# Query numbers of 16 of 25 edge groups: gathered by GpSimd from DRAM instead of selected on TensorE and VectorE

## The chip, the cores and the metric

The kernel runs on one core of a Trainium2 chip. The metric is the device time of that core in microseconds (us), the median over several runs. Engines are named as the profile does: PE (TensorE), DVE (VectorE), ACT (ScalarE), POOL (GpSimd) and SP (SyncE, which here only issues DMAs and reads registers).

## The reference: what is computed

Two layers of a relational graph attention network run over 3125 nodes of 768 features and 53125 edges (with one loop per node); each edge has one of three types. After them come a residual and a layer norm:

```python
xr = jnp.einsum('nd,rdf->rnf', x, W)        # every node's features by every relation's weights
oi = xr[etype, dst]; oj = xr[etype, src]
qi = oi @ q; kj = oj @ k
alpha = jax.nn.leaky_relu(qi + kj, NEG_SLOPE)
e = jnp.exp(alpha - segment_max(alpha, dst)[dst])
a = e / (segment_sum(e, dst)[dst] + EPS)
out = segment_sum(a * oj, dst) + b          # by head; 4 heads in layer 1, one in layer 2
```

The edges come sorted by their target `dst`. The term `qi` depends on an edge's target and its type alone: for each edge of layer 1 it is 4 numbers (one per head), taken from a table of 3125 nodes x 3 relations x 4 heads. How each edge gets its 4 numbers is what the change is about.

## The kernel before

The edges are cut into 25 groups (NB) of whole target nodes, at most 128 nodes each. A group has 17 slots (SL; 14 in the first, SLF) of 128 edges, one edge per partition. The kernel has three stages. The first stage multiplies x by layer 1's weights. The second gathers the products' rows by edge, weighs and sums them per node, and multiplies by layer 2's weights. The third does the same for layer 2's edges and ends with the norm.

**The products of the first stage.** The products of x and W1 are made 128 nodes at a time, in 6 pieces of up to 398 columns; the last piece carries, beside features, the 12 query numbers (4 heads x 3 relations) of each node. A piece is 18 matmuls (six blocks of features, high and low parts) into one of two PSUM banks. `d_row` (L579) empties the bank: ACT copies it (L581), SP stores it to the table `tab1`. For the last piece DVE also splits the 12 query numbers into three bf16 parts (`split3`, L586), which SP stores to `q1_d` in DRAM.

**The order of the work.** `phase1` (L601) is written as a list of steps: `when(n, f, ...)` puts work at step n, and one piece of the products runs at each step, so a node group has six steps. The order on each engine is exactly the order of these calls; there is no scheduler behind it. At a step the listed work is issued first, then the piece's matmuls, then `d_row` of the piece before. Work that waits on an engine holds up all that stands behind it on that engine.

**Indices.** `a_index`, `a_index2` and `c_next` (L608 to L653) read the edge list of group b at steps 5b+11 and 5b+12, turn it so that each edge sits on its partition, and leave in SBUF the row number for the gathers (`ridx`), the target's place within the group (`dl`) and the type (`rel`).

**Query numbers before.** For each group b, SP loads the targets of all 2176 edges broadcast over 128 partitions (`s_load1`, 544 KB into `sT`) and the group's 128 rows of `q1_d` (`q_load1`). DVE compares `sT` with each partition's node number (`a_q`, L680), which gives one-hot columns in bf16. PE multiplies each slot's one-hot block by the 36 query parts of the nodes (`a_q2`, 17 small matmuls, tile `pq`). DVE makes a one-hot of the type (`a_oh`, L686), multiplies (L708) and sums (L711) into `pall[:, b]`, the 4 numbers of each edge. The second stage's `alpha` (L874) adds them to the key numbers.

**What else hangs on GpSimd in this stage.** 18 blocks of layer 2's weights W2 are prepared on the way. `w_load(i)` at step 12 + 6i issues one or two loads from GpSimd into the single buffer `share[3]` (L745). `w_split(i)` two steps later copies the block's high part on ACT (L752), subtracts on DVE for the low part (L753) and makes two products with q2 and k2 on DVE (L756); the copies are there for blocks 0 to 11 only. Blocks 4 to 11 are stored by a DMA from GpSimd (L759), blocks 0 to 3 by SP. The next load waits until DVE is done with the buffer. After the first stage GpSimd issues all the gathers of table rows (L468), 128 rows of 3,088 bytes per instruction.

The lines that fix where things stand:

```python
k = (q, q, q, q + 3, q + 3, q + 4, q + 5)      # q = max(c + 1, 6 * b + 2), c = 10 + 5 * b
for n, f in zip(k, (s_load1, q_at, q_load1, a_q, a_oh, a_q2, a_q3)):
    when(n, f, b)
...
when(6 * (2 + i), w_load, i)
when(6 * (2 + i) + 2, w_split, i)
```

Of the kernel before, what the change touches and what calls it, by code (L numbers as in the profile page):

```python
# [9 lines left out]
F32 = mybir.dt.float32  # L10
# [3 lines left out]
I32 = mybir.dt.int32  # L14
AF = mybir.ActivationFunctionType
ALU = mybir.AluOpType
# [5 lines left out]
P = 128  # L22
# [4 lines left out]
BIG = float(2**100)  # L27
# [35 lines left out]
def _index(ap):  # L63
    return bass.IndirectOffsetOnAxis(ap=ap, axis=0)
# [3 lines left out]
SL = 17  # L68
# [41 lines left out]
def kernel(  # L110
# [21 lines left out]
    nc = tc.nc  # L132
    N, D = x.shape
    R = layers[0]["W"].shape[0]
    E = src.shape[0]
    NB = (N + P - 1) // P
    NP = NB * P
# [3 lines left out]
    H1 = l1["H"]  # L141
# [5 lines left out]
    HW = RW // 2  # L147
    EARLY = 6
    GB = NB - 4
# [4 lines left out]
    V, S, G, T = nc.vector, nc.scalar, nc.gpsimd, Counted(nc.tensor)  # L154
    OOB = float(1 << 20)

    dram = ctx.enter_context(tc.tile_pool(name="fdram", bufs=1, space=DRAM))
# [6 lines left out]
    tab2 = dram.tile([NP * R, RW], F32, name="ftab2")  # L164
    xb_d = dram.tile([NP + P, D], F32, name="xb_d")
    q1_d = dram.tile([NP + P, H1 * R * 3], BF, name="q1_d")
    w2_d = dram.tile([R * DT * P, 2 * D], F32, name="w2_d")

    ident = keep.tile([P, P], F32, name="fident")
# [26 lines left out]
    pall = keep.tile([P, NB, SL, H1], F32, name="pall")  # L196
# [258 lines left out]
    def slots(b):  # L455
        return SL if b else SLF
# [122 lines left out]
    def d_row(o, q, b, p, po):  # L579

        S.copy(o[:, :HW], po[:, :HW])  # L581
        to = tab1[b * P * R:(b + 1) * P * R, :].rearrange("(p r) f -> p r f", r=R)
        nc.sync.dma_start(to[:, p // 2, p % 2 * HW:(p % 2 + 1) * HW], o[:, :HW])
        if p == len(PIECES1) - 1:
            q1s = q.tile([P, H1 * R, 3], BF, name="q1s", bufs=2)
            split3([q1s[:, :, i] for i in range(3)], po[:, HW:HW + H1 * R], q, [P, H1 * R])  # L586
            nc.sync.dma_start(q1_d[b * P:(b + 1) * P, :], q1s.rearrange("p k s -> p (k s)"))

    def stretches(rows, at_, a, e):

# [10 lines left out]
    def phase1(pre, work, psum, left, due, more):  # L601
        st = a_st
# [13 lines left out]
        def a_index2(b):  # L616
            pT = st[b]["pi"]
            c = SL
            V.tensor_scalar(dl[:, b, :], pT[:, c:2 * c], 1.0 / BIG, n_all[:, b:b + 1], op0=ALU.mult,
                            op1=ALU.subtract)  # L620
            inv = work.tile([P, SL], F32, name="inv", bufs=2)
            V.tensor_scalar(inv, dl[:, b, :], float(P), OOB, op0=ALU.is_ge, op1=ALU.mult)
            V.tensor_add(ridx[:, b, :], pT[:, 0:SL], inv)
            if b in first_rows:
                V.tensor_scalar(rfirst[:, first_rows[b], :], ridx[:, b, :], NP * R - 1, None, op0=ALU.min)
            V.tensor_copy(rel[:, b, :], pT[:, 2 * c:3 * c])

        counts = work.tile([32, 32], F32, name="counts", bufs=1)
        V.memset(counts, 0.0)
# [52 lines left out]

        def a_oh(b):
            s = st[b]
            s["oh"] = work.tile([P, SL, R * 3], F32, name="oh", bufs=2)
            V.tensor_tensor(s["oh"], rel[:, b, :, None].to_broadcast([P, SL, R * 3]),  # L686
                            rel3.rearrange("p r s -> p (r s)")[:, None, :].to_broadcast([P, SL, R * 3]),
                            op=ALU.is_equal)
# [81 lines left out]
        def when(n, f, *a):  # L770
            ev.setdefault(n, []).append((f, a))

        TAIL = 6 * (GB - 1)
        S0 = 10
        when(8, pad_rows)
        for b in range(NB):
            c = S0 + 5 * b
            when(c - 3 if b else S0 - 1, c_load, work, b)
# [4 lines left out]
            q = max(c + 1, 6 * b + 2)  # L783
            if b < GB:
                k = (q, q, q, q + 3, q + 3, q + 4, q + 5)
            else:
                q = max(c + 2, 6 * GB + 4 + 2 * (b - GB))
                e = 6 * NB - 5 + b - GB
                k = (q, 6 * NB - 14 + b - GB, 6 * NB - 5, q + 5, e, e, e)
            for n, f in zip(k, (s_load1, q_at, q_load1, a_q, a_oh, a_q2, a_q3)):  # L790
                when(n, f, b)
            if b > 1:
                t, e = {2: (2, 4), 3: (3, 10), GB: (TAIL - 8, TAIL - 3), GB + 1: (TAIL - 7, TAIL), GB + 2: (TAIL - 6, TAIL - 2), GB + 3: (TAIL - 5, TAIL - 1)}.get(
                    b, (6 * b - 11, 6 * b - 8))
# [1345 lines left out]
```

## Time and profile before

| | |
|---|---|
| time, median of 3 runs | 1773.26 us (1772.15 to 1775.79) |
| the profiled execution | 1773.27 us, span 1771.5 us |
| PE, DVE, ACT, POOL busy | 1649.9, 1122.2, 434.6, 903.6 us |
| mean granted clock of PE | 0.974 |
| from 100 to 400 us: PE, DVE, ACT, POOL busy of 300 us | 300.0, 202.6, 63.6, 15.2 |
| small query products in the first stage (`pq`) | 425 recorded, 177 to 213 ns each by record, pipelined |
| first gather of the second stage begins at | 534.4 us |

The span runs from the first to the last instruction of the profiled execution. A row of the page's second part cuts the span into 40 slices of 44.3 us; the first stage takes the first twelve. A row of a timeline gives start, length, engine, line, operation and tiles, and in brackets how long the engine sat idle before it and what ended that. A row of the groups by line gives the count, then busy time and mean length, then idle time before and what ended it. "SPq" and the like is the engine's instruction queue, where DMAs are issued.

### The profile page before, as it was taken

How to read it: one execution, taken by the hardware profiler on the slowest of the kernel's cores; microseconds unless marked ns; L12 is line 12 of the kernel's file. 1: busy time of each engine (PE TensorE's matmuls, PEld its weight loads, DVE VectorE, ACT ScalarE, POOL GpSimd, SP SyncE). 2: the span in 40 equal slices, each digit the busy share in tenths (PEclk: the TensorE clock that was granted, in tenths of full speed). 3: DMA queues.
4: the chain of work that ended last, by engine and by line, in shares of the span. 5: the costliest groups of instructions: out<-in, count | busy, mean ns of one | idle time of the engine just before them, and what ended most of it. 6: DMA issues, size and time to landing. Idle time of an engine off the chain costs nothing. (4 is left out here: it accounts for less than half of the span.)

```text
span 1771.5 us, 38682 instructions
## 1 busy us (share of the span) xinstructions
PE 1649.9 (93%) x14093; PEld 1272.7 (72%) x14093; DVE 1122.2 (63%) x3912; ACT 434.6 (25%) x803; POOL 903.6 (51%) x907
## 2 busy tenths in 40 slices
PE   8999999999993999999999999938999999999996
PEld 8899999999992788888888888813444444444443
DVE  7566677566425666666677777366666666666662
ACT  6222222111210112221121221102333333333331
POOL 4100000000007777777777776067777777777750
PEclk9999999999996999999999999968999999999998
DMA  7576667556578999999999998478999999999960
GB/s 258 189 242 225 213 219 238 202 169 211 180 260 279 335 347 356 349 351 355 348 341 351 347 347 297 144 259 305 330 338 334 342 336 334 336 337 334 336 224 28
DMA packets 169366, 501.53 MB, mean 283 GB/s; under 512 B 39890, under 2 KB 82489, under 8 KB 169166
## 3 DMA queue, kind: packets, MB, share of 16 engines
q0 software_dynamic: 70832, 343.91, 54.9%
q1 hardware_dynamic: 90104, 144.97, 24.6%
q10 hardware_dynamic: 8230, 10.10, 1.7%
q8 instruction: 112, 1.84, 0.4%
q14 instruction: 88, 0.72, 0.1%
HBM read 414.04 MB, written 89.63 MB: 284 GB/s over the span
## 5 line engine op out<-in xcount | busy, mean ns | idle before, releaser
L468 POOL DMA_INDIRECT extra<-ftab,ridx x296 | 302.7, 1023 | 93.4 <-issue 53.0
L53 PE MATMUL po<-waH,hT 128*128 128x386 f32 (+1 forms) x1200 | 326.4, 347 | 1.4 <-DVE hT L1031 0.7
L53 PE MATMUL po<-waH,xT 128*128 128x386 f32 x1104 | 293.7, 342 | 0.9 <-ACT xT L255 0.4
L468 POOL DMA_INDIRECT share<-ftab,ridx x204 | 207.1, 1015 | 66.9 <-issue 38.9
L53 PEld LDWEIGHTS po<-waH,hT 128*128 128x128 f32 x1200 | 216.7, 189 | 4.8 <-DVE hT L1031 1.1
L53 PE MATMUL D<-extra,AT 128*128 128x512 f32 (+1 forms) x600 | 217.8, 501 | 1.3 <-ACT AT L1400 1.3
L53 PEld LDWEIGHTS po<-waH,xT 128*128 128x128 f32 x1104 | 203.1, 189 | 1.4 <-DVE xT L256 0.7
L53 PE MATMUL po<-waL,hT 128*128 128x386 f32 (+1 forms) x600 | 203.1, 339 | 0.0
L53 PE MATMUL po<-waL,xT 128*128 128x386 f32 x552 | 187.9, 340 | 3.1 <-DVE wbH L416 3.0
L581 ACT COPY share<-po 128x386 f32<-128x386 f32 x150 | 72.2, 481 | 369.5 <-PE po L53 305.0
L53 PEld LDWEIGHTS D<-extra,AT 128*128 128x128 f32 x600 | 107.1, 191 | 73.0 <-issue 65.4
L53 PE MATMUL acc<-waH,marks 128*32 128x386 f32 (+1 forms) x868 | 152.7, 494 | 0.7 <-DVE marks L1320 0.7
L53 PE MATMUL acc<-waL,marks 128*32 128x384 f32 (+1 forms) x848 | 151.7, 498 | 0.0
L53 PE MATMUL po<-wbH,xT 128*128 128x386 f32 (+1 forms) x552 | 147.6, 342 | 0.9 <-DVE g L410 0.9
L53 PE MATMUL acc<-extra,sel 128*32 128x193 f32 x2736 | 124.9, 335 | 2.3 <-DVE sel L940 2.3
L468 POOL DMA_INDIRECT waL<-ftab,ridx x108 | 109.0, 1010 | 32.9 <-issue 27.1
L468 POOL DMA_INDIRECT waH<-ftab,ridx x104 | 105.1, 1010 | 31.7 <-issue 25.3
L53 PE MATMUL acc<-extra,marks 128*32 128x384 f32 (+1 forms) x568 | 116.0, 492 | 0.0
L53 PEld LDWEIGHTS po<-waL,hT 128*128 128x128 f32 x600 | 113.4, 189 | 0.0
L53 PEld LDWEIGHTS acc<-extra,sel 128*32 128x32 f32 x2736 | 87.8, 112 | 31.3 <-issue 5.1
L745 POOL DMA_DIRECT2D share<-in_L_gnn_W_dram x24 | 12.8, 537 | 188.5 <-DVE w2j L756 117.0
L53 PE MATMUL acc<-share,marks 128*32 128x386 f32 (+1 forms) x428 | 108.8, 488 | 0.0
(286 smaller groups left out, 2981.7 us busy)
## 6 DMA issues: line engine op xcount, KB each, us to landing
ftab<-share SPq DMA_DIRECT2D x150, 193.0 KB
ftab<-r SPq DMA_DIRECT2D x50, 386.0 KB
sT<-dr_d SPq DMA_DIRECT2D x23, 544.0 KB
xb_d<-share SPq DMA_DIRECT2D x25, 384.0 KB
ftab<-y SPq DMA_DIRECT2D x100, 96.0 KB
share<-xb_d SPq DMA_DIRECT2D x25, 384.0 KB
share<-in_x_dram SPq DMA_DIRECT2D x24, 384.0 KB
out_dram<-share SPq DMA_DIRECT2D x24, 384.0 KB
```

The source lines that it names most:

```text
L53: return self.add(self.engine.matmul(to, weights, moving, **more), to, moving)
L468: return G.indirect_dma_start(out=to, out_offset=None, in_=tab, in_offset=_index(i[:, j:j + 1]), bounds_check=NP * R - 1, oob_is_err=False)
L581: S.copy(o[:, :HW], po[:, :HW])
L745: G.dma_start(w2[i][p:p + n], l2["W"][r, at:at + n, :])
```

## The change

For groups b below 20 with b % 5 != 4 (16 groups: 0 to 3, 5 to 8, 10 to 13, 15 to 18), the one-hot path is left out: no `s_load1`, `q_at`, `q_load1`, `a_q`, `a_oh`, `a_q2`, `a_q3`. Instead:

- Every node group's 12 query numbers are also copied in float32 with the relation outermost (`q1f`), and stored by SP as 3 rows of 4 numbers per node to a new DRAM table `q1r_d`.
- `a_index2` makes for the 16 groups one more index, target x 3 + type, moved out of range for an edge that is not the group's.
- Per slot one indirect DMA on GpSimd reads 128 rows of 16 bytes from `q1r_d` straight into `pall[:, b, j, :]`. Out-of-range edges are skipped, which is why `pall` is cleared first, at step 8.
- The gathers of a group stand at steps max(6b+9, c+3) to 6 later, two or three to a step. At a step that also has a `w_load` or `w_split`, the gathers stand ahead of it.
- The type's one-hot `oh` has one buffer instead of two.

```diff
+    q1r_d = dram.tile([NP * R, H1], F32, name="q1r_d")
...
+            q1f = q.tile([P, R, H1], F32, name="q1f", bufs=2)
+            V.tensor_copy(q1f, po[:, HW:HW + H1 * R].rearrange("p (h r) -> p r h", h=H1))
+            nc.sync.dma_start(q1r_d[b * P * R:(b + 1) * P * R, :].rearrange("(p r) h -> p r h", r=R), q1f)
...
+            if by_gather(b):
+                d = work.tile([P, SL], F32, name="qd", bufs=2)
+                V.scalar_tensor_tensor(d, pT[:, c:2 * c], R / BIG, pT[:, 2 * c:3 * c], op0=ALU.mult, op1=ALU.add)
+                st[b]["qi"] = work.tile([P, SL], I32, name="qi", bufs=7)
+                V.tensor_add(st[b]["qi"], d, inv)
+
+        def by_gather(b):
+            return b < GB - 1 and b % 5 != 4
+
+        def q_gather(b, j):
+            n = (b + 1) * P * R
+            G.indirect_dma_start(out=pall[:, b, j, :], out_offset=None, in_=q1r_d[:n, :],
+                                 in_offset=_index(st[b]["qi"][:, j:j + 1]), bounds_check=n - 1, oob_is_err=False)
...
-            s["oh"] = work.tile([P, SL, R * 3], F32, name="oh", bufs=2)
+            s["oh"] = work.tile([P, SL, R * 3], F32, name="oh", bufs=1)
...
+        when(8, G.memset, pall, 0.0)
...
-            for n, f in zip(k, (s_load1, q_at, q_load1, a_q, a_oh, a_q2, a_q3)):
-                when(n, f, b)
+            if by_gather(b):
+                for j in range(slots(b)):
+                    when(max(6 * b + 9, c + 3) + j * 7 // SL, q_gather, b, j)
+            else:
+                for n, f in zip(k, (s_load1, q_at, q_load1, a_q, a_oh, a_q2, a_q3)):
+                    when(n, f, b)
```

## The prediction

> **What bounds the kernel now.** I read the page's share lines first, then the windows view cut by stage, and then, inside the first stage, the timelines of PE, ScalarE, VectorE and GpSimd. The chain of waits begins near 1140 us, so it says nothing of the stage that is changed; only two of its rows serve below, for how long a gather takes to land. A measurement of this kernel tells a change from none at about 0.2%, 3.5 us.
>
> ```profile
> span 1771.5 us, 38682 instructions
> PE   8999999999993999999999999938999999999996
> POOL 4100000000007777777777776067777777777750
> 100.00:400.00 300.00, 300.00 (x1932) 297.22 (x1931) 202.58 (x723) 63.62 (x118) 15.19 (x29) 1.00 0.67 217
> 700.00:1140.00 440.00, 436.36 (x5104) 378.35 (x5103) 304.85 (x857) 88.63 (x192) 303.23 (x297) 1.00 0.93 331
> ```
>
> The two last rows give, for a stretch, the busy time of PE, its weight loads, DVE, ACT and POOL, then the granted clock, the DMA share and GB/s. From 100 to 400 us, inside the first stage, PE has no idle time at a clock of 1.00. VectorE is busy 203 of 300 us and GpSimd 15. So what the change takes from VectorE is worth nothing by itself, and what it takes from PE counts in full, as long as nothing new makes PE wait. GpSimd looks free, and that is what has to be tested.
>
> **What PE is spared.** Per gathered group 17 small products go.
>
> ```profile
> 189.92 0.34 PE L53 MATMUL po<-waH,xT 128*128 128x386 f32 x1
> 190.10 0.59 PE L53 MATMUL pq<-q,sT 128*128 128x36 bf16 x17
> 190.54 0.43 PE L53 MATMUL po<-wbH,xT 128*128 128x386 f32 x1
> 220.22 0.48 ACT L581 COPY share<-po 128x386 f32<-128x386 f32 x1 [2.71 <-PE po L53]
> 220.59 0.84 ACT L752 CAST w2hl<-share 128x768 fp32r<-128x768 f32 x1
> 223.38 0.48 ACT L581 COPY share<-po 128x386 f32<-128x386 f32 x1 [1.95 <-issue]
> 227.06 0.48 ACT L581 COPY share<-po 128x386 f32<-128x386 f32 x1 [3.20 <-PE po L53]
> ```
>
> The 17 run from 190.10 to 190.54, 0.44 us. These are rows of the timelines of PE and ScalarE. ScalarE's copies of finished pieces, which follow PE, stand 3.16 us apart in the first pair (220.22 to 223.38) and 3.68 in the next, which holds such a set: 0.5 us. I take 0.49: 16 x 0.49 = 7.9 us, at least 16 x 0.44 = 7.0. If nothing else mattered, the profiled execution's own time, 1773.27 us (1.8 around its span, and the median of the runs but for 0.01), would become 1765.4.
>
> **What VectorE and SP get.**
>
> ```profile
> L680 DVE TENSOR_SCALAR sT<-sT,cols 128x2176 bf16<-128x2176 bf16 x22 | 17.1, 777 | 1.5 <-DMA sT<-dr_d 1.5
> L708 DVE TENSOR_TENSOR tq<-pq,oh 128x324 f32<-128x324 f32 (+1 forms) x42 | 18.0, 469 | 8.1 <-PE pq L53 8.1
> L711 DVE TENSOR_REDUCE pall<-tq 128x68 f32<-128x612 f32 x21 | 16.6, 791 | 0.7
> L686 DVE TENSOR_TENSOR oh<-rel,rel 128x153 f32<-128x153 f32 x21 | 6.6, 314 | 0.0
> 98.23 0.17 DVE L626 COPY rel<-pi 128x17 f32<-128x17 f32 x1
> 98.86 0.18 DVE L207 CAST q1s<-po 128x12 bf16<-128x12 f32 x1 [0.46 <-ACT share L581]
> ```
>
> A gathered group loses 0.78 + 2 x 0.47 + 0.79 + 0.31 = 2.8 us of VectorE. It gains two 17-wide operations like the last but one row (0.2 us each), and every group gains one copy of 12 numbers (0.2 us). All of that lies under PE, as VectorE is a third idle. The new copy reads the product bank after the five steps of the split, so the bank comes free some 0.6 us later; PE wants it one piece, 3.2 us, after the product ended, and this eats slack only (nothing; up to 0.3 us a group, 7 us, where VectorE is late anyway). SP loses 32 loads, and gains 25 stores of about 0.35 us of issue: nothing. The clearing of the gathered numbers (1,700 a partition, on GpSimd) stands ahead of the first weight load; that load is issued at 88.8 us and first read at 101.9, which covers it.
>
> **What GpSimd gets.** 16 groups x 17, less 3 for the short first one: 269 indirect gathers.
>
> ```profile
> 535.79 1.05 POOL L468 DMA_INDIRECT share<-ftab,rfirst  x1 [0.30 <-issue]
> 537.14 1.00 POOL L468 DMA_INDIRECT share<-ftab,rfirst  x1 [0.31 <-issue]
> 538.44 1.00 POOL L468 DMA_INDIRECT share<-ftab,rfirst  x1 [0.30 <-DMA share<-ftab,rfirst]
> L468 POOL DMA_INDIRECT extra<-ftab,ridx x296 | 302.7, 1023 | 93.4 <-issue 53.0
> 36.51 0.53 POOL L288 DMA_DIRECT2D dr_d<-padb  x1
> 185.19 1.05 POOL L745 DMA_DIRECT2D share<-in_L_gnn_W_dram  x2 [1.04 <-DVE w2j L756]
> 202.99 0.57 POOL L759 DMA_DIRECT2D w_d<-w2hl  x1 [16.75 <-DVE w2hl L753]
> ```
>
> The trace has no gather of 16-byte rows. Its gathers of 3,088-byte rows start 1.30 us apart when nothing holds them (537.14 to 538.44): 1.00 of work and a gap of 0.30; over 296 of them work and gap make (302.7 + 93.4) / 296 = 1.34. GpSimd's plain DMAs take about 0.53 us whether they move half a kilobyte (dr_d) or 384 KB (in two halves, L745), so the bytes of a row should not matter, but the instruction. Bounds for one gather: 0.53 (a plain one) and 1.34. I take 1.30, because it is the same instruction with the same 128 indices. 17 x 1.30 = 22.1 us a group.
>
> The next rows are from the groups by line, the timelines and the chain of waits. A group of products takes PE
>
> ```profile
> L752 ACT CAST w2hl<-share x12: 836/837/837, 101.9 to 319.5; 128x768 fp32r<-128x768 f32 x12
> 161.50 0.84 ACT L752 CAST w2hl<-share 128x768 fp32r<-128x768 f32 x1
> 187.71 0.96 DVE L732 TENSOR_TENSOR share<-share 128x768 f32<-128x768 f32 x1 [1.90 <-DMA share<-in_x_dram]
> 183.30 0.35 SPq L728 DMA_DIRECT2D share<-in_x_dram  x1
> 1174.34 4.53 DMA waL<-ftab,rfirst
> 1240.77 6.38 DMA waL<-ftab,ridx
> ```
>
> (319.5 - 101.9) / 11 = 19.8 us, and 19.3 once the small products are gone. So in four groups of five GpSimd needs more time than PE. It can't make it up ahead, for GpSimd's queue also holds the loads of W2's blocks (L745) and, for blocks 4 to 11, the stores of their parts (L759). What queues behind a late load: ScalarE's copy of block i (L752), which stands in ScalarE's order ahead of the copies that empty the product banks, and those hold PE, which has two banks. The copy of 220.59 could start as late as about 225.3 (bank wanted at 226.5, less 0.84 and 0.48, which overlap by 0.1): it may be 4.7 us late before PE stalls. A load of 384 KB takes 4.4 us from issue to use (183.30 to 187.71), and gathers of 395 KB took 4.5 and 6.4; I take 4.8.
>
> Burst one, groups 0 to 3. GpSimd can begin when group 0's index is made, 98.4 plus the two new operations, 98.8. By the steps of the diff 14 + 17 + 17 gathers and the first 8 of group 3, and the loads of blocks 1 and 2, precede the load of block 3: 56 x 1.30 + 2 x 0.53 = 73.9. With 0.5 for the load and 4.8 to land, block 3 is there at 178.0. Its copy stood at 161.5; four sets of small products less make that 159.5. It is 18.5 late, less 4.7: PE has lost 13.8 us. Group 4 gathers nothing, and GpSimd catches up.
>
> Burst two, groups 5 to 8. From here GpSimd waits for the high and low parts of block i before it stores them, which stops it from running ahead:
>
> ```profile
> POOL w_d L759 <- DVE w2hl L753: 119.9, 7, 22.1
> POOL share L745 <- DVE w2j L756: 117.0, 13, 19.5
> ```
>
> From one copy to the next: 1.9 us until the parts are there (0.84 + 0.96 and a little), 0.6 store, 12 gathers 15.6 (two of group i, ten of the next), 0.5 load, 4.8 landing: 23.4 against 19.3, 4.1 late each time. The first of the burst has 10 gathers and a load in two parts: 21.3, 2.0 late. Copies 5 to 8 are late by 2.0, 6.1, 10.2 and 14.3; less 4.7, PE loses 9.6.
>
> Burst three, groups 10 to 13: copies 10 and 11 are late by 2.5 and 6.6, so 1.9 lost. Blocks 12 to 17 have neither store nor ScalarE copy. Lateness reaches PE there through VectorE alone, which must split the next features within five pieces (16 us), with about 8 us of other work before; it is 12 late by block 13: 3 us more (0 to 4). After the pause at group 14 GpSimd can run ahead, and burst four costs nothing. It is through with the gathers some 45 us before the second stage's first gather, which waits for the table as before.
>
> Sum: 13.8 + 9.6 + 1.9 + 3 = 28.3 lost, 7.9 won: 20.4 slower, **1793.7, say 1794 us**. Every 1 us of landing moves it by about 7 (1 in burst one, 4 in two, 2 in three), every 0.01 us of gather period by about 1.4, as some 140 gathers stand inside the late stretches.
>
> SBUF — State Buffer, section "Who interferes with whom", of the Trainium skill says that a VectorE copy, cast or tensor_scalar in a two-port mode locks GpSimd out for its whole length, so that GpSimd's descriptors wait. By that rule the gathers in a stage with many casts would be longer than I take them. In the second stage, with VectorE busy 305 of 440 us, the mean is 1.023 us against 1.00 in the quiet rows, which agrees with a small effect; the 0.02 would add some 3 us.
>
> **The rivals.**
>
> 1. The gather of short rows is cheaper and GpSimd keeps up. Place: the same queue; decided by the gather's period. By 1.4 us for every 0.01 the loss equals the gain at about 1.30 - 0.15 = 1.15 us, and at 1.00 the stalls are gone: 1773.3 - 7.9 = 1765.4, faster. For it: there is no row of this size in the trace, and the gap of 0.30 is put down to nothing the profile shows. Against it: the plain DMAs' 0.53 at both sizes.
>
> 2. Gathers are dearer in this stage. 128 packets more each: in a window of the trace with small packets only on the hardware queue,
>
> ```profile
> q1 hardware_dynamic: 840, 0.23, 4.8%
> ```
>
> over 22 us (534 to 556), a packet of 274 bytes costs 0.048 x 16 x 22 / 840 = 20 ns, so a gather takes 128 x 20 / 16 = 0.16 us of each DMA engine, an eighth of its period. With a DMA share of 0.67 and the 544 KB loads gone, that fits, so I hold this for unlikely. At 1.50 us a gather the sum is 20.4 + 28 and more, as burst four then stalls too: about 1825.
>
> 3. The lateness is absorbed in part (landing 4 us, period 1.2): loss and gain nearly cancel, 1770 to 1781.
>
> 4. The change doesn't do what it says: a store of the table waits for earlier gathers to have read it, SP stands still behind it, and the groups run one after the other. 22 us of gathering in place of 3 of cover in 16 groups would be hundreds of us. Each gather reads only rows up to its own group's end, and later stores lie past them, so I give it almost nothing.
>
> **How the numbers follow.** My forecast (late by the sum above, 1781 to 1812) has 0.58. Rival 1 has 0.20, rival 2 has 0.09, rival 3 has 0.12, half of it within 3.5 us of before and the rest slower, rival 4 has 0.01. Faster is rival 1 with a little of 3, 0.21; same 0.07; slower 0.72. The bounds of landing (4.4 to 6.4) give 1791 to 1805, those of the period with the locks 1794 to 1800 above and 1765 below. To leave out no more than 2 in 10 the range goes down to rival 1's time and up to 1812: 1765 to 1812. The forecast's own is 1781 to 1812.
>
> **What would show it.** Right: in the changed kernel's windows PE falls below full busy time between 120 and 310 us and again near 350, with ScalarE's cast L752 waiting for the DMA into share and PE for the banks; gathers start 1.30 us apart; L752's twelve casts span more than 217.6 us; full PE after some 410 us. Wrong: GpSimd idle between groups, gathers 1.15 us apart or less, L752's casts 19.3 us apart, PE full throughout; then the time is near 1765. If PE stalls to the stage's end, rival 2 holds. The second and third stage should keep their lengths.

## The result and the profile after

The changed kernel takes 1820.24 us (1817.56 to 1820.95) beside 1773.78 (1772.15 to 1776.09) for the kernel before: a ratio of 1.0255, 95% interval 1.0244 to 1.0267. It is 46 us slower. The forecast had the sign, the place and the mechanism, and less than half of the size (20.4 us); the time lies 8 us above the top of its range (1812).

First the page's share lines of the changed kernel and its windows, which answer those of before (per stretch: busy time of PE, weight loads, DVE, ACT and POOL, granted clock, DMA share, GB/s).

```profile
span 1818.8 us, 38573 instructions
PE   8997988999996699999999999938999999999995
POOL 4167675777722777777777777147777777777740
100.00:400.00 300.00, 272.01 (x1495) 268.97 (x1494) 152.42 (x610) 56.30 (x105) 219.48 (x214) 0.94 0.59 173
700.00:1140.00 440.00, 436.54 (x5156) 377.49 (x5148) 311.31 (x881) 86.76 (x189) 333.27 (x325) 1.00 0.97 348
```

VectorE fell from 203 to 152 us in the stretch and GpSimd rose from 15 to 219, as meant. PE lost 28 of 300 us and a part of its clock (1.00 to 0.94). The second stage is as before. Now the waits of the changed kernel from 100 to 500 us (total, times, longest):

```profile
ACT w2hl L771 <- DMA share<-in_L_gnn_W_dram: 65.3, 9, 11.6
PE po L53 <- ACT share L582: 27.6, 7, 7.1
POOL w_d L778 <- DVE w2hl L772: 21.7, 4, 11.5
```

L771 is the copy of a W2 block that was L752 before, L764 its load (L745), L778 its store (L759), L582 the copy that empties a bank (L581). ScalarE waits 65 us for loads that come late, and behind it PE waits 28 us for banks. The copies by ScalarE's timeline, for the first two bursts, then the group of all twelve:

```profile
104.27 0.84 ACT L771 CAST w2hl<-share 128x768 fp32r<-128x768 f32 x1
182.52 0.83 ACT L771 CAST w2hl<-share 128x768 fp32r<-128x768 f32 x1 [11.64 <-DMA share<-in_L_gnn_W_dram]
200.57 0.84 ACT L771 CAST w2hl<-share 128x768 fp32r<-128x768 f32 x1
223.84 0.83 ACT L771 CAST w2hl<-share 128x768 fp32r<-128x768 f32 x1 [3.37 <-DMA share<-in_L_gnn_W_dram]
247.38 0.83 ACT L771 CAST w2hl<-share 128x768 fp32r<-128x768 f32 x1 [7.75 <-DMA share<-in_L_gnn_W_dram]
273.99 0.83 ACT L771 CAST w2hl<-share 128x768 fp32r<-128x768 f32 x1 [8.98 <-DMA share<-in_L_gnn_W_dram]
297.92 0.83 ACT L771 CAST w2hl<-share 128x768 fp32r<-128x768 f32 x1 [7.01 <-DMA share<-in_L_gnn_W_dram]
314.23 0.84 ACT L771 CAST w2hl<-share 128x768 fp32r<-128x768 f32 x1
489.44 0.83 ACT L256 CAST w2hl<-xr 128x768 fp32r<-128x768 f32 x1
...
L771 ACT CAST w2hl<-share x12: 831/832/837, 104.3 to 360.5; 128x768 fp32r<-128x768 f32 x12
```

The twelve span 256.3 us, against 217.6 before. The row of 489.44 is another copy, of features, near the end of the stage, and serves as a second mark. Cut at such marks, the 47.3 us between the two spans lie here:

| stretch | before | after | difference |
|---|---|---|---|
| start to first W2 copy | 101.9 | 104.3 | +2.4 |
| first to twelfth W2 copy | 217.6 | 256.3 | +38.7 |
| to the copy of features (L255, now L256) | 127.6 | 128.9 | +1.3 |
| to the second stage's first gather | 87.2 | 85.7 | -1.5 |
| second stage | 622.1 | 624.3 | +2.2 |
| third stage, to the start of the last instruction | 607.2 | 605.5 | -1.6 |
| from there to the end of the span | 7.9 | 13.8 | +5.9 |

So 41 us belong to the first stage and 6 to a place nobody looked at, behind the last instruction. Last, PE at its longest stall and the windows around it, in the changed kernel:

```profile
176.33 0.34 PE L53 MATMUL po<-waH,xT 128*128 128x386 f32 x1
183.78 0.69 PE L53 MATMUL po<-waH,xT 128*128 128x386 f32 x1 [7.11 <-ACT share L582]
184.27 0.53 PE L53 MATMUL po<-waL,xT 128*128 128x386 f32 x1
...
170.00:180.00 10.00, 6.67 (x38) 6.35 (x36) 3.06 (x19) 0.48 (x1) 7.61 (x9) 0.98 0.61 159
180.00:190.00 10.00, 6.21 (x20) 6.22 (x21) 5.46 (x9) 2.33 (x4) 8.12 (x7) 0.51 0.54 162
```

After a wait of 7.11 us the matmuls take 0.53 instead of 0.34 us, and the granted clock in that window is 0.51. The page "TensorE: Matmul & The Clock Gate" of the Trainium skill, Part 1, says that PE falls to half clock after an idle window of about 3.4 us and needs about as long a busy one to come back; the trace agrees in kind. What that costs is not what it seems, as the fourth experiment shows.

### The profile page after: what moved, and what is told of

Read it like the earlier page. It is cut to its first block, busy times and chain, and to the rows that moved or that the text cites. A ratio compares the mean times of both kernels' runs of the same rounds, so it can differ in the third digit from the quotient of the medians.

```text
span 1818.8 us, 38573 instructions
## 1 busy us (share of the span) xinstructions
PE 1658.6 (91%) x13821; PEld 1281.0 (70%) x13821; DVE 1088.2 (60%) x3889; ACT 433.9 (24%) x803; POOL 1196.8 (66%) x1177
## 5 line engine op out<-in xcount | busy, mean ns | idle before, releaser
L644 POOL DMA_INDIRECT pall<-q1r_d,qi x269 | 289.8, 1077 | 91.4 <-issue 79.3
L53 PE MATMUL po<-waH,xT 128*128 128x386 f32 x1104 | 306.8, 354 | 31.1 <-ACT share L582 27.6
L53 PEld LDWEIGHTS po<-waH,xT 128*128 128x128 f32 x1104 | 213.9, 199 | 34.5 <-ACT share L582 29.8
L53 PE MATMUL po<-waL,xT 128*128 128x386 f32 x552 | 194.6, 353 | 2.9 <-DVE wbH L417 2.9
L582 ACT COPY share<-po 128x386 f32<-128x386 f32 x150 | 71.5, 482 | 342.3 <-PE po L53 264.6
L469 POOL DMA_INDIRECT waH<-ftab,ridx x104 | 104.6, 1006 | 31.7 <-issue 24.7
L53 PEld LDWEIGHTS po<-waL,hT 128*128 128x128 f32 x600 | 113.3, 189 | 0.0
L53 PEld LDWEIGHTS po<-waL,xT 128*128 128x128 f32 x552 | 110.3, 200 | 3.2 <-POOL wbL L380 3.2
```

The costliest lines, as they stand in the source:

```text
L53: return self.add(self.engine.matmul(to, weights, moving, **more), to, moving)
L469: return G.indirect_dma_start(out=to, out_offset=None, in_=tab, in_offset=_index(i[:, j:j + 1]), bounds_check=NP * R - 1, oob_is_err=False)
L644: G.indirect_dma_start(out=pall[:, b, j, :], out_offset=None, in_=q1r_d[:n, :], in_offset=_index(st[b]["qi"][:, j:j + 1]), bounds_check=n ...
```

## The experiments

The theory is the prediction's: GpSimd's one queue sets the pace of a burst, since the loads and stores of W2 stand in it between gathers. The rivals are the gathers' DMA traffic, PE's falling clock as a cause of its own, and things beside the gathers. Each run stands beside the kernel before on the same chip, and ratios are to it. Two of the chips used run the kernel before in 2023 to 2028 us instead of 1775; what was measured on those is told apart.

### 1. W2 loads and stores moved to SP

```diff
-                G.dma_start(w2[i][p:p + n], l2["W"][r, at:at + n, :])
+                nc.sync.dma_start(w2[i][p:p + n], l2["W"][r, at:at + n, :])
...
-                (G if i >= 4 else nc.sync).dma_start(w2_d[i * P:(i + 1) * P, :]..., hl.bitcast(F32))
+                nc.sync.dma_start(w2_d[i * P:(i + 1) * P, :]..., hl.bitcast(F32))
```

> The changed kernel, with W2's block loads and stores issued by SP instead of GpSimd; the 269 gathers stay on GpSimd as they are. Queue theory (the loss is W2's loads coming late because they stand behind gathers on GpSimd): nothing on ScalarE or PE waits for GpSimd any more, PE is busy throughout the first stage at a clock of 1.00, and the 7.9 us of small products are won: about 1766 to 1768, the first gather of the second stage near 527. Traffic theory (the 34,000 packets of 16 bytes hold up the other transfers, or the gathers hold up VectorE): the gathers are all still there, so most of the loss stays: 1805 to 1820.

Measured: 1772.7 us, ratio 0.998 (0.9967 to 0.9992). The same 269 gathers, and the loss is gone. Its window from 100 to 500 us:

```profile
100.00:500.00 400.00, 398.91 (x2318) 397.18 (x2317) 227.02 (x926) 84.40 (x157) 293.02 (x269) 1.00 0.68 199
```

PE is full at a clock of 1.00 while GpSimd gathers 293 us. So neither the gathers' packets nor their landing hurt; what stood behind them did. It came out some 5 us above what was expected: one part is that the first W2 load came late (SP issued it at 105.7, the copy followed at 113.3), another that behind the last instruction 9.8 us pass instead of before's 6.8 (experiment 8).

### 2. Only the stores moved to SP

Of the edit above, the second part alone:

```diff
-                (G if i >= 4 else nc.sync).dma_start(w2_d[i * P:(i + 1) * P, :]..., hl.bitcast(F32))
+                nc.sync.dma_start(w2_d[i * P:(i + 1) * P, :]..., hl.bitcast(F32))
```

> The W2 stores on SP and the loads on GpSimd again, for a chip on which the kernel before takes about 1775. The theory of one queue: 1790 to 1800, between the changed kernel and the one with loads and stores on SP (1773). If the late loads alone decide, 1812 to 1820. If the stores' waits alone decide, 1772 to 1776. On the chip where the kernel before takes 2028 it came to 1.088 of it, with SP's own transfers issued late, which no theory had; if that belongs to the kernel and not to the chip, it shows here as gaps between SP's issues without a wait, and over 1830.

Measured: 1804.08 us, ratio 1.0158 (1.0143 to 1.0173): 28 us over the kernel before instead of 46. Waits and copies of this kernel:

```profile
ACT w2hl L771 <- DMA share<-in_L_gnn_W_dram: 52.1, 7, 11.1
...
218.60 0.83 ACT L771 CAST w2hl<-share 128x768 fp32r<-128x768 f32 x1 [2.07 <-DMA share<-in_L_gnn_W_dram]
289.64 0.83 ACT L771 CAST w2hl<-share 128x768 fp32r<-128x768 f32 x1 [7.04 <-DMA share<-in_L_gnn_W_dram]
305.88 0.84 ACT L771 CAST w2hl<-share 128x768 fp32r<-128x768 f32 x1
325.04 0.84 ACT L771 CAST w2hl<-share 128x768 fp32r<-128x768 f32 x1
```

Burst one is as it was, since its stores were on SP already. In burst two the copies stand 23.7 us apart, (289.64 - 218.60) / 3, instead of 24.7, and burst three is not late at all. The stores carry some 18 us, by the wait in front of them: of the 21.7 us that GpSimd waited before stores in the changed kernel, 8.8 fall in the fifth group and 11.5 in the tenth. Without that wait it runs ahead there and has a lead for the next burst: it begins the gathers of group 10 at 297.3 us instead of 317.2. The late loads carry the rest. Neither alone is the cause. The expected time (1790 to 1800) was a little low.

### 3. GpSimd's time alone, without a gather

The kernel before, with work of GpSimd alone at the places of the gathers:

```diff
+        def hold(b, j):
+            if j == 0:
+                G.tensor_copy(idle[:, 0:1], rel[:, b, 0:1])
+            for _ in range(4):
+                G.memset(idle, 0.0)          # idle: 128 x 232, float32
...
+        for b in range(NB):
+            if b < GB - 1 and b % 5 != 4:
+                c = S0 + 5 * b
+                for j in range(slots(b)):
+                    when(max(6 * b + 9, c + 3) + j * 7 // SL, hold, b, j)
```

A first size, five clears of 272 numbers, came out longer than a gather:

> The kernel before (one-hot selection kept, no gather in the first stage), with GpSimd kept busy in the gathers' places: for each of the 269 gathers five clears of 272 numbers of a spare buffer, about 1.3 us together; the first of a group waits for the group's index. No DMA is added. Queue theory: W2's loads are as late as in the changed kernel, so the stalls return, without the 7.9 us that the small products save: 1800 to 1828 by how close the clears come to the gathers' 1.38 us. Traffic theory: no packets, so no loss: 1772 to 1777.

Measured: 1948.29 us, ratio 1.0983 (1.0952 to 1.1014). A place took 1.95 us of GpSimd, not a gather's 1.38. It shows that clears of SBUF without one packet stall PE; the size says nothing yet. With four clears of 232:

> The matched clears again, for a chip on which the kernel before takes about 1775: the kernel before with four clears of 232 numbers on GpSimd, 1.38 us, at each place where the changed kernel has a gather; the clears' results are not used. On the chip where it takes 2028 this came to 1.029 of the kernel before. If GpSimd's queue time alone makes the loss: 1810 to 1822. If the gathers' packets, or the longer gathers beside the W2 loads, carry a good part of it: 1785 to 1800.

Measured: 1830.49 us, ratio 1.0312 (1.0295 to 1.0329). The clears by group, ScalarE's wait for W2 and the span of the twelve copies:

```profile
L775 POOL MEMSET idle<- 128x232 f32 x1076 | 324.5, 302 | 60.6
...
ACT w2hl L752 <- DMA share<-in_L_gnn_W_dram: 76.3, 9, 12.3
...
L752 ACT CAST w2hl<-share x12: 831/832/837, 100.6 to 368.1; 128x768 fp32r<-128x768 f32 x12
```

A place takes (324.5 + 60.6) / 269 = 1.43 us, not the 1.38 aimed at, and the loss is 54 us, above the 1810 to 1822 that were expected. At 0.05 us a place over the gathers' 1.38, the prediction's slope (1.4 us for every 0.01) takes 7 us off: 47, against the gathers' 46. This kernel keeps the small products, which are worth 8.5 us (experiment 7), and has neither the additions (2 us) nor the longer end (5.9 us) of experiment 8. These nearly cancel, so the two losses may be compared as they stand. GpSimd's time in the queue is enough to make the whole loss. This is the prediction's mechanism, shown without a gather.

### 4. PE's clock held up

The changed kernel with 156 matmuls whose result is not used, put at the steps where PE stalls:

```diff
+        FILL = {21: 6, 27: 30, 33: 38, 51: 18, 57: 24, 63: 12, 81: 18, 97: 10}
+        held = psum.tile([P, 512], F32, name="held", bufs=1)
...
+            for _ in range(FILL.get(n, 0)):
+                T.matmul(held[:, :P], ident, ident, start=True, stop=True)
```

> The changed kernel, with dummy matmuls (156 in all, into a bank that nobody reads) put on PE just ahead of the pieces before which PE stalled, to fill about four fifths of each stall; the result is the same. If the clock that falls after each stall costs time of its own: the granted clock stays near 1.00 between 100 and 450 us and the time falls by about 9 us (the stretches from the last late copy of a burst to the next burst), to about 1811; not by the full 16 us by which the matmuls were slower, because inside a burst GpSimd's chain sets the pace whatever PE does. If the clock is a symptom only: 1818 to 1821. If the dummies are in the way: above 1822.

Measured: 1816.73 us, ratio 1.0243 (1.0214 to 1.0272), which overlaps the changed kernel's 1.0255 (1.0244 to 1.0267). The time lies between the two expectations, 1811 and 1818 to 1821. From 150 to 200 us, and two of its copies:

```profile
150.00:200.00 50.00, 49.60 (x345) 49.15 (x344) 24.36 (x91) 9.24 (x17) 34.93 (x34) 1.00 0.55 154
...
182.32 0.83 ACT L771 CAST w2hl<-share 128x768 fp32r<-128x768 f32 x1 [12.38 <-DMA share<-in_L_gnn_W_dram]
198.01 0.84 ACT L771 CAST w2hl<-share 128x768 fp32r<-128x768 f32 x1
```

The clock is 1.00 where it was 0.83, and the copy at the end of burst one comes at 182.32 instead of 182.52. Inside a burst GpSimd's chain sets the pace, and a faster PE only waits longer. Between bursts the clock counts: the next copy follows after 15.7 us instead of 18.1. By the copy of features this kernel is 3.1 us ahead. An accounting of the changed kernel's profile, 30 us of idle PE from 100 to 500 and 5% of 370 us at a lower clock, would have put 18 us down to the clock. The held clock won back 3 of them, so that would have been wrong.

### 5. Every other group

The changed kernel with gathers in groups 0, 2, ... 18 alone:

```diff
-            return b < GB - 1 and b % 5 != 4
+            return b < GB - 1 and b % 2 == 0
```

> The changed kernel with the gathers in every second group only (10 groups: 0, 2, ... 18) instead of four of five. Queue theory: between two W2 loads stand at most 14 gathers and after a store at most 10 before the next load, so no copy is later than the 4.7 us that PE bears: no stall, 10 x 0.49 = 4.9 us won, less up to 2: 1769 to 1771. Traffic theory: the loss shrinks with the number of gathers, by 10/16: about 1773 + 29 = 1802.

Measured: 1777.91 us, ratio 1.0011 (0.9994 to 1.0028). PE is busy 398.75 of the 400 us at a clock of 1.00, so with every second group free GpSimd catches up and nothing stalls, as expected. From the first W2 copy to the copy of features it is 3.9 us shorter than before, which is 0.4 us for each of ten groups. The time is 7 us above the expected 1769 to 1771, and 6 of these are again the stretch behind the last instruction, 12.9 us.

### 6. What lengthens a gather

The prediction took 1.30 us for a gather, from quiet rows. The groups by line of the changed kernel have 1.08 of work and, without the 9.6 us before the first, 0.30 of gap:

```profile
L644 POOL DMA_INDIRECT pall<-q1r_d,qi x269 | 289.8, 1077 | 91.4 <-issue 79.3 <-PE po L53 9.6 <-DMA pall<-q1r_d,qi 1.2
L644 POOL DMA_INDIRECT pall<-q1r_d,qi x269: 992/998/1754, 101.0 to 511.5; - x135
```

The median is 0.998, the longest 1.75: some are far longer. I first put them down to the W2 loads that drain in the same queue, but in the kernel of experiment 1, with those on SP, the mean is 1.089:

```profile
L644 POOL DMA_INDIRECT pall<-q1r_d,qi x269 | 293.0, 1089 | 96.2 <-issue 76.5 <-DMA ftab<-share 14.2 <-DMA pall<-q1r_d,qi 2.4
```

In the changed kernel GpSimd's and VectorE's timelines side by side show something else:

```profile
226.58 0.96 DVE L775 SCALAR_TENSOR_TENSOR w2j<-share,kq 128x768 bf16<-128x768 f32 x1
226.85 1.61 POOL L644 DMA_INDIRECT pall<-q1r_d,qi  x1 [0.30 <-issue]
228.76 1.00 POOL L644 DMA_INDIRECT pall<-q1r_d,qi  x1 [0.30 <-issue]
232.36 0.96 DVE L257 TENSOR_TENSOR xT<-share,xT 128x768 fp32r<-128x768 f32 x1
232.67 1.53 POOL L644 DMA_INDIRECT pall<-q1r_d,qi  x1 [0.30 <-issue]
```

Of the changed kernel's 269 gathers 44 take over 1.1 us, and 43 of these begin inside a VectorE operation over 768 numbers a partition with two inputs in SBUF (L775, L751, L772, L257); eight others begin so and are short. Of these 51, 49 end 0.87 to 0.95 us after that operation's end; the two others began within 0.04 us of its start and were not held. The 181 that meet no such operation have a mean of 1.008. A coincidence in time is no cause yet, so one kind of these operations was replaced by passes with one input and the same width, which leaves out layer 2's key and query numbers:

```diff
-                V.scalar_tensor_tensor(j, w, 1.0, kq2[:, s, :], op0=ALU.mult, op1=ALU.mult,
-                                       accum_out=wkq2[:, t, (Q2 if s else K2)[r]:][:, 0:1])
+                V.tensor_scalar(j, w, 1.0, 0.0, op0=ALU.mult, op1=ALU.add,
+                                accum_out=wkq2[:, t, (Q2 if s else K2)[r]:][:, 0:1])
```

> The changed kernel with the 36 two-input products of W2's blocks replaced by one-input passes of the same width, again, for a chip on which the kernel before takes about 1775; layer 2's key and query numbers are not computed. If two SBUF inputs hold the gathers up, the mean of a gather is about 1.04 us and the time 1813 to 1817; else 1.07 to 1.08 us and 1818 to 1821.

Measured: 1815.65 us, ratio 1.0223 (1.0202 to 1.0245), 0.0032 or some 5.7 us below the changed kernel's; the two intervals just touch. The gathers of this kernel and the replaced operations beside them:

```profile
L644 POOL DMA_INDIRECT pall<-q1r_d,qi x269 | 281.3, 1046 | 91.4 <-issue 78.9 <-PE po L53 9.7 <-DMA pall<-q1r_d,qi 1.5
...
223.19 0.95 DVE L775 TENSOR_SCALAR_CACHE_REDUCE w2j<-share 128x768 bf16<-128x768 f32 x1
223.47 1.05 POOL L644 DMA_INDIRECT pall<-q1r_d,qi  x1 [0.31 <-issue]
```

The new passes take the same 0.95 us, and of 24 gathers that begin inside one a single one is long (mean 1.02), where it was 15 of 19 (mean 1.44). Beside the other two-input operations the gathers stay long. So a VectorE operation with two SBUF inputs holds an indirect DMA on GpSimd until it is done. A second input is not the only thing that does: the 44th long gather (at 504.52, 1.44 us) began inside the compare of `sT` (L699, a single wide input of 2176 bf16 numbers), and of 20 gathers in nine kernels that began inside one, 18 end 0.86 to 0.92 us after it. No run replaced that operation. SBUF — State Buffer of the Trainium skill, section "Who interferes with whom", states that a VectorE instruction with two SBUF inputs contends with a GpSimd instruction that reads SBUF, and infers that descriptor generation is not met by it since it needs the write side only. The first half agrees with these rows (1.44 against 1.02 us). The inference is not tested by them, since a gather also reads its row numbers from SBUF.

### 7. Loads and stores on SP, and 18 groups

W2's stores and loads on SP, the first load left on GpSimd, and 18 groups gathered instead of 16:

```diff
-            return b < GB - 1 and b % 5 != 4
+            return b < GB - 1 and b % 10 != 9
...
-                G.dma_start(w2[i][p:p + n], l2["W"][r, at:at + n, :])
+                (nc.sync if i else G).dma_start(w2[i][p:p + n], l2["W"][r, at:at + n, :])
```

> W2 loads and stores on SP, the first load on GpSimd, 18 groups gathered, again, for a chip on which the kernel before takes about 1775. By the theory of one queue 1767 to 1771. If the late end of the gathers holds the second stage's start, 1774 to 1785. On the chip where the kernel before takes 2028 it came to 1.118 of it; if that belongs to the kernel and not to the chip, over 1850.

Measured: 1772.62 us beside 1776.25, ratio 0.9981 (0.9971 to 0.9992). Two copies, the window, and the end:

```profile
120.90 0.84 ACT L771 CAST w2hl<-share 128x768 fp32r<-128x768 f32 x1
140.05 0.84 ACT L771 CAST w2hl<-share 128x768 fp32r<-128x768 f32 x1
...
100.00:500.00 400.00, 399.84 (x2299) 399.05 (x2298) 222.11 (x901) 84.80 (x158) 312.24 (x288) 1.00 0.69 202
...
1756.18 1.04 POOL L1508 DMA_INDIRECT out_dram<-share,oidx  x1 [51.64 <-ACT share L1505]
```

A gathered group takes 19.15 us from copy to copy. Before, the eleven intervals between the twelve copies make 217.6 us and hold 13 sets of small products, so a set costs (217.6 - 11 x 19.15) / 13 = 0.53 us (0.49 was forecast). From the first W2 copy to the copy of features it is 335.7 us against 345.2, 9.5 shorter, which is 18 times 0.53. But its span is 1770.7 us, so 13.5 us pass behind the last instruction instead of 6.8, and 3 us are left, which is what the times show (3.6). The expected 1767 to 1771 left that end out. The ratio is no better than experiment 1's 0.998, whose interval overlaps.

### 8. The additions, and the stretch behind the last instruction

The changed kernel with all groups selected as before, while the copies `q1f`, their stores, the new index and the clear of `pall` stay:

```diff
-            if by_gather(b):
-                for j in range(slots(b)):
-                    when(max(6 * b + 9, c + 3) + j * 7 // SL, q_gather, b, j)
-            else:
-                for n, f in zip(k, (s_load1, q_at, q_load1, a_q, a_oh, a_q2, a_q3)):
-                    when(n, f, b)
+            for n, f in zip(k, (s_load1, q_at, q_load1, a_q, a_oh, a_q2, a_q3)):
+                when(n, f, b)
```

> The changed kernel without its gathers again, all 25 groups selected as before, with the float32 copies, their stores, the row numbers and the clear kept, for a chip on which the kernel before takes about 1775. If the additions cost nothing: 1772 to 1777, with before's 6.8 us from the last instruction's end to the span's end. If the tail of 12.8 us comes with the added stores and not with the gathers, 1778 to 1783.

Measured: 1778.49 us beside 1776.25, ratio 1.0011 (1.0001 to 1.0021). Between the marks in the first stage it is 1.8 us longer than before. So the additions cost about 2 us, and its end is that of before:

```profile
span 1777.6 us, 38791 instructions
1769.80 1.04 POOL L1504 DMA_INDIRECT out_dram<-share,oidx  x1 [51.66 <-ACT share L1501]
```

That leaves 1777.6 - 1770.84 = 6.8 us. The changed kernel has

```profile
1804.97 1.03 POOL L1508 DMA_INDIRECT out_dram<-share,oidx  x1 [51.11 <-ACT share L1505]
```

and 12.8 us. The kernels without an added gather have 6.7 or 6.8, and those with 167 or more have 9.8 to 13.5. To that kernel the gathers were given back at places where nobody waits, writing again what was selected: the 17 of one group, then the 102 of six.

```diff
+            if b == 16:                              # g2: if by_gather(b) and b >= 12
+                for j in range(slots(b)):
+                    when(6 * b + 9 + j * 7 // SL, q_gather, b, j)
```

> The kernel with the added stores and without gathers (1778.5 beside 1776.3 for the kernel before), with the 17 gathers of one group put back behind that group's selection, at a place where no W2 load is left on GpSimd; they write again what was selected. PE should not stall. If any added gather brings the longer tail, the time from the last instruction's end to the span's end is 9 us or more and the time 1780 to 1786. If the tail grows with the number of gathers, 7.0 to 7.3 us and 1776 to 1779. If the tail belongs to something else in the kernels with gathers, 6.8.

> The same with the gathers of six groups, some 100 of them, behind all W2 loads. If the tail is a step, 9 to 13.5 us as with 170 to 303 gathers, and 1780 to 1786. If it grows with their number (6 us for 170 to 303), 8 to 10 us and 1778 to 1782. If it belongs to something else, 6.8 us and 1776 to 1779.

Measured: 1780.09 us, ratio 1.0026 (1.0015 to 1.0037), and 1780.62 us, ratio 1.0034 (1.0019 to 1.0048). Their ends are 8.6 us with 17 gathers and 6.4 with 102. That is neither a step nor a slope, and no expectation holds for both. It goes with the program: the same kernel on another chip has the same end (13.5 and 13.4; 11.8 and 11.7). No engine and almost no DMA is busy in it, but GpSimd's queue is: its instructions at the last line stand there (minimum, median and maximum in ns), in the kernel before and in the changed one.

```profile
L2130 POOLq DRAIN  x3: 50/109/2600, 1768.0 to 1771.2; - x3
...
L2154 POOLq DRAIN  x3: 50/109/7255, 1810.7 to 1818.5; - x3
```

The longest DRAIN grew from 2.60 to 7.25 us, and the INC_SWDGE_SEM ahead of it from 0.82 to 1.96: 5.8 of the 5.9 us. With 0, 17, 102, 167 and 269 added gathers the DRAIN takes 2.60, 3.99, 2.19, 7.58 and 7.25 us. An estimate from these five, a rise of 0.083 us a gather and a fall of 8.85 us at every 107th or so, gives 2.60, 4.0, 2.2, 7.6 and 7.2: a sawtooth over the number of DMAs that GpSimd has issued. It is a fit, no run was made to test it, and what the instruction waits for stays open.

### 9. The same kernels on other chips

Experiments 2, 3, 6, 7 and 8 were also run on chips where the kernel before takes 2028 us (experiment 6: 2023).

> The kernel before, with its one-hot products kept, and at each place where the changed kernel has a gather four clears of 232 numbers on GpSimd (some 0.30 us each with 0.05 between them, 1.38 us a place, which is the mean period of the changed kernel's gathers); the clears' results are not used. The earlier run with 1.9 us a place overshot. If GpSimd's queue time alone makes the loss, the chain of a group is the changed kernel's (24 to 25 us) and the first stage ends 35 to 45 us later than before: 1810 to 1822. If the gathers' packets, or the longer gathers beside the W2 loads, carry a good part of it, less: 1785 to 1800.

> The changed kernel with the W2 stores issued by SP and the W2 loads left on GpSimd behind the gathers. The theory of one queue: the store's wait for the split no longer stands in front of the next gathers, so a group's chain on GpSimd is 17 gathers of 1.36 and two loads, less the wait of some 5 us behind the copy in each period: 1790 to 1800, between the changed kernel and the one with loads and stores on SP (1773). If the late loads alone decide, it stays at 1812 to 1820. If the stores' waits alone decide, it falls to 1772 to 1776.

> W2 loads and stores on SP, the first load left on GpSimd so that the first copy is not late, and 18 groups gathered instead of 16 (all of the first 20 but the tenth and the twentieth). 18 times 17 gathers of 1.37 us are 419 us from 101, so GpSimd is done at 520, ahead of the stage's end at 530. By the theory of one queue the PE never waits for a copy: two more groups save 2 times 0.49 us, the first copy's lateness goes, and it comes 4 to 8 us below before: 1767 to 1771. If the late end of the gathers holds the second stage's start, 1774 to 1785.

> The changed kernel without its gathers: all 25 groups selected on TensorE and VectorE as before, while the float32 copies of the query numbers, their stores to the DRAM table, the row numbers and the clear of the target stay. It prices the additions beside the gathers. If they cost nothing: 1772 to 1777, and the time between the last instruction's end and the span's end is before's 6.8 us. If the tail of 12.8 us comes with the added stores and not with the gathers, 1778 to 1783.

> The changed kernel with VectorE's 36 products of a W2 block with k2 and q2 (two inputs in SBUF, 0.95 us each) replaced by as many passes over the block alone, which sum it (one input, same width, same sum output); so layer 2's key and query numbers are not computed. If operations with two SBUF inputs hold the gathers up: of 44 long gathers some 22 go, the mean falls from 1.077 to 1.04 us, and by the forecast's slope (1.4 us for every 0.01) the time falls by about 5 us to 1813 to 1817. If the loads in the queue or the DMA traffic make them long: 40 or more stay and the time is 1818 to 1821.

> The control: the same replacement in the kernel before, which has no gathers in that stage; layer 2's key and query numbers are not computed here either. VectorE is idle a third of that stage, so by every theory 1772 to 1778.

| kernel | ratio there | ratio on the usual chip |
|---|---|---|
| matched clears | 1.0294 (1.0221 to 1.0367) | 1.0312 |
| stores on SP | 1.0875 (1.0785 to 1.0965) | 1.0158 |
| 18 groups, loads and stores on SP | 1.1176 (1.111 to 1.1241) | 0.9981 |
| additions without gathers | 0.9938 (0.9885 to 0.9991) | 1.0011 |
| one input, with gathers | 1.0741 (1.0657 to 1.0826) | 1.0223 |

The control, one input in the kernel before, takes 2021.45 us there beside 2022.92. Without gathers the ratios agree with those of the usual chip or nearly so; with gathers they don't. The loss is in the first stage: in the control the second stage's first gather begins at 535 us, as on the usual chip, but in the version with 18 groups at 754 instead of 525. The fastest version is the slowest there. Its window, then SP's timeline and the group of its semaphore instructions at the table's stores (minimum, median and maximum in ns):

```profile
100.00:500.00 400.00, 259.57 (x1308) 252.29 (x1307) 134.40 (x541) 51.81 (x96) 226.22 (x218) 0.81 0.41 118
...
205.28 0.32 SPq L584 DMA_DIRECT2D ftab<-share  x1
211.03 0.70 SPq L512 DMA_DIRECT2D nx<-ed_d  x1
215.93 0.70 SPq L514 DMA_DIRECT2D dw<-ed_d  x1
...
L584 SPq EVENT_SEMAPHORE  x141: 3/17/699, 29.1 to 750.2; - x141
```

On the usual chip these two small loads are issued 0.43 to 0.63 us apart and no semaphore instruction of that group takes over 17 ns. Here the pair shown stands 4.9 us apart with nothing waited for, the widest of 25 (one more is over 2, six are 1.3 to 1.5), and some semaphore instructions take 0.7 us. So on these chips SP itself runs slowly at times while GpSimd gathers, and there the gathers do harm beside GpSimd's queue. Why, the profile doesn't show.

## Why the prediction was wrong, and where it was right

- **The bound, and the place of the loss: right.** PE is below full busy time from 120 to 310 us, again near 360, and a little at 418; the copies wait for their load and PE for its banks. Experiments 1, 2 and 3 show the mechanism. Rival 1 falls (a quiet gather is 1.30 apart, not 1.15), rival 3 with it, and rival 4 has no row. Rival 2's "dearer gathers" holds in kind, but not by packets.
- **"28.3 lost": too small in each burst.** By the copies shown above, with 19.15 us for a group that gathers and 0.53 for a set of small products that stays, PE's work lost 19.2 us in burst one (13.8 forecast), 17.4 in burst two (9.6) and about 12 from there to the copy of features (4.9): 48.5 in all. For the last the measure is the 167.0 us that the kernel before takes there, less seven sets. That PE's idle time from 100 to 500 us is 30.4 (369.6 of 400 busy), near the forecast, is luck: the other 18 us are matmuls at a clock of 0.95 instead of 1.00.
- **"I take 1.30" for a gather: the step that failed most.** It measured 1.38. The row was right, but it came from a quiet stretch. The prediction named the rule on VectorE's locks, looked at casts alone and at the second stage's mean (1.023), and put 3 us to it outside the sum. By its own slope 0.08 us is 11 us; experiment 6 took 0.03 away and measured 5.7 where the slope gives 4, by which 0.08 would be 14.
- **Burst two's chain of 23.4: the wrong path, and too short.** Measured 24.7, (297.92 - 223.84) / 3. The prediction's chain goes from copy to copy, with GpSimd waiting for the split before each store. Within the burst it waited 1.1, 0, 0.4 and 0 us there: what set the pace was GpSimd's own time. An estimate of that is 17 x 1.38, a load and a store, 0.6 each with a gap of 0.3: 25.3; its stores stand 24.9 apart.
- **A load's 5.3 (0.5 and 4.8 to land): too long.** The nine late copies begin 4.4 us after their load is issued, on average. This error goes the other way.
- **"19.3 once the small products are gone": 19.15.** The mean of 19.8 holds 13 sets in 11 intervals, and one was taken off.
- **"Less 4.7" for every burst: only partly there.** After burst one the copies made up 1.1 us (18.05 apart instead of 19.15), after burst two 2.8. PE came out of each stall at a low clock: with the clock held it was 3.5 after burst one. This is the part of the clock that counts, some 3 us, and the prediction had no term for it.
- **Additions at nothing: about 2 us** (experiment 8). **PE spared 7.9: nearly right**, at 0.53 a group 8.5.
- **Nothing behind the last instruction: 5.9 us**, with no term at all; it is GpSimd's DRAIN and the instruction ahead of it.

The two profiled executions differ by 47.3 us, 27 more than forecast. 20 of these are the bursts' lost time and 6 the end. Of the 20, the period makes 11 to 14 and the clock some 3. The rest isn't assigned, as these overlap and come from different runs. "The second and third stage should keep their lengths" held: 2.2 us more and 1.6 less.

## What to carry to other kernels

An engine that is nearly idle is free only for work that nobody queues behind: look at what else stands in its queue, and compare its time per period with that of the engine that sets the pace, before filling it to the brim. A duration from a quiet stretch is a lower bound where another engine can hold the instruction up, so take it from a stretch with the same neighbours. And idle time and lost clock in a profile are symptoms: what they are worth shows when one is taken away.

## What the runs showed that was not expected

- An indirect DMA on GpSimd that begins while VectorE multiplies two inputs of 768 numbers from SBUF takes 1.44 us on average instead of 1.00; beside a one-input pass of the same length 1.02. The held ones end 0.87 to 0.95 us after VectorE's operation does.
- Holding PE's clock at 1.00 through stalls of up to 7 us moved the total by 0.0012, within its interval.
- From the last instruction to the end of the span pass 6.4 to 13.5 us, by the program and not by the chip. GpSimd's DRAIN fills 2.2 to 8.0 of them, and fits a sawtooth over the DMAs that it has issued.
- On two chips SP issued loads up to 5 us apart with nothing waited for while GpSimd gathered, and the version that wins by 0.2% on the usual chip loses 12%.
